# A transformer block with windowed attention: all query blocks through transposed scores, and both feed-forward biases as row products

## The chip, the cores and the metric

The kernel runs on one core of a Trainium2 chip. A core has four compute engines with a queue each: TensorE (PE in the profile; its weight loads are listed apart, as PEld), VectorE (DVE), ScalarE (ACT) and GpSimd (POOL). SyncE (SP) computes nothing here and issues almost all DMAs, in order. The metric is the device time of one execution in microseconds, the median over repeated runs.

## The reference

The input x is 4 sequences of 2048 tokens with 256 channels. What is computed, cut to what matters:

```python
def attn(h):                      # 16 heads of 16 channels, window of 64 keys, causal
    q, k, v = proj(h, Wq), proj(h, Wk), proj(h, Wv)
    bias = where((j <= i) & (j > i - 64), 0, -inf)
    a = softmax(q @ k.T * 0.25 + bias)
    return (a @ v) @ Wo.T

def ffn(h):                       # 1024 hidden units, weights quantized to -1, 0, 1
    return relu(h @ quantize(W1).T + b1) @ quantize(W2).T + b2

x = x + attn(layernorm(x))
x = x + ffn(layernorm(x))
```

Everything is in 32-bit floats. The kernel gets that accuracy from half-precision matmuls by splitting each operand into a high part and a low part (the value minus its high part).

## The kernel before

The 8192 tokens are worked in 32 chunks of 256 (C). A chunk has four query blocks (NB) of 64 tokens, numbered 0 to 3; with the window of 64, a block sees the keys of its own block and of the one before. Heads go in eight pairs (NP).

For each chunk:

- **load** and **norm_in** bring in a chunk (xt), normalize it (layernorm) and transpose its parts by a DMA transpose (xT).
- **project** makes q, k and v. The parts of q and k go to DRAM (qd, kd), and **stack** reads them back into qst and kst so that the rows of one pair of heads lie together for a matmul. The query stack keeps the four blocks interleaved: its columns are in the order (query, block). Three pairs of stacks stand in rotation (NQ), and a pair is loaded again once the chunk three before has signalled "used".
- **scores** computes a block's scores with queries on the rows (sp), eight matmuls of 128 columns. The two key blocks are laid into one half: slot t holds the key of the earlier block where that is still in the window, and otherwise the newer one (copy_predicated, L698). This is the ring order.

From here the blocks take one of two ways. RINGS (L39) says that blocks 0 and 2 of each chunk take the ring path and 1 and 3 the plain one.

- **Ring path, ring_weights (L747 to L793).** VectorE takes the row maxima (L753). The exponentials are made either by one subtraction on VectorE (L764) and one activation (L766), or by eight activations with a bias of their own (L761). ScalarE casts the high part (rh, L771), VectorE or GpSimd subtracts for the low part. VectorE multiplies both parts with two masks that put each slot back to the earlier or the newer key block (pm, L777), and SyncE issues a DMA transpose (pt, L787) that gives the weights with keys on the rows. The stack's use is signalled once for a block, early, behind the scores.
- **Plain path, maxima (L711) and weights (L795).** The row maxima of the chunk's plain blocks are gathered, scaled (mh), transposed on TensorE (L729), copied by ScalarE (mst, L733, one small copy for each block), written to DRAM (md) by a DMA that ScalarE issues and read back by one that GpSimd issues into row 96 of the query stack (L738). Then the scores are computed once more, transposed, with keys on the rows: for a group of four pairs a mask product of 512 columns (L803) and four products of 128 columns whose moving operand is the interleaved query stack (L806). The row maximum is subtracted by the product itself. ScalarE takes the exponential and the high part; the low part is made by GpSimd (L816, L819, L821) or by VectorE out of PSUM (L825, L827, L829). There are two groups to a block, and each signals the stack's use.

**values** (L834) multiplies the weights of a block, from ph and pl or from pt, with v in 24 small products. **wo_out** divides, transposes by DMA, applies Wo, adds to xt and normalizes again. **ffn1** (L955) computes one 128-wide slice of the hidden layer for two chunks together (26 chunks; the last six go one by one), **ffn2** (L1007) the output of a chunk, 32 products, then the sum with xt and the store.

The biases are handled in ffn1 and wo_out:

- First bias: with "folded" false, ScalarE adds it in the ReLU (r, L999), casts the high part (hh, L1002), and the low part is a subtraction on VectorE or GpSimd (hl, L552). With "folded" true, a product with a row of ones puts it into the sum on TensorE (L973), ScalarE makes the ReLU straight into half precision (L991), and VectorE makes the low part out of PSUM (L993).
- Second bias: GpSimd adds it to xt (L944), or TensorE adds it by a row product (L1023).

What sets the order: each piece of work is a generator that says which engine takes it and for about how long. A planner (class Lanes) runs these at build time; of the pieces that could start first, the one with the lowest number goes on (PRIO). The order of issue on each engine that comes out is fixed in the program. **lanes.pick** takes, of several ways to do something, the one that loads the engines most evenly by the planner's own costs; in the program before it never takes "folded", and never TensorE for the second bias.

PSUM: the score tiles sp have two buffers, and all other products share four banks in rotation (BUFS "bank"). The low parts that two engines can make are all in one helper (low, L552), so the profile shows them under one line and tells them apart by their tiles.

Of the kernel before, what the change touches and what calls it, by code (L numbers as in the profile page):

```python
# [23 lines left out]
W = 64  # L24
# [14 lines left out]
RINGS = ((0, 2),)  # L39
RING0 = ()  # L40
NRING0 = 0
PRIO = {'norm': -1.1, 'proj': 0.4, 'max': 0.2, 'att': 2.9, 'val': -2.2, 'wo': 0.6, 'ffn': 5.5, 'ffn2': 5.6, 'prep': 3.6}
BUFS = {'xt': 9, 'ln': 2, 'xT': 3, 'zT': 2, 'qk': 4, 'vp': 4, 'pp': 4, 'op': 2, 'av': 2, 'o': 1, 'h': 10, 'r': 7, 'rh': 1, 'pm': 2, 'pt': 2, 'bank': 4, 'lin': 6, 'sp': 2, 'tp': 3, 'pv': 4}
# [9 lines left out]
class Lanes:  # L53
    """Order of issue: the tasks are generators that say before each piece of work which engine takes it and for
    about how long; of those that could start first, the one with the lowest number goes on. Tasks also wait
    for each other's signals and for buffers."""
# [36 lines left out]
    def pick(self, options):  # L93
        """Of several ways to do something, the one that loads the engines most evenly."""
        top = max(self.load[e] * WT[e] for e in "PADG")
        cost = [sum(t * math.exp((self.load[e] * WT[e] - top) / TAU) for e, t in o) for o in options]
        return cost.index(min(cost))
# [15 lines left out]
    def chain(self, n):  # L113
        """The engines keep the order of issue."""
# [12 lines left out]
    def tensor(self, start, t):  # L127
        """The tensor engine's time for work of t: its clock is halved after a window with little work."""
# [73 lines left out]
def kernel(ctx: ExitStack, tc: tile.TileContext, x, Wq, Wk, Wv, Wo, W1, b1, W2, b2, out):  # L202
# [26 lines left out]
    rhp = pool("rhp", BUFS["rh"])  # L229
    pmp = pool("pmp", BUFS["pm"])  # L230
    ptp = pool("ptp", BUFS["pt"])
# [23 lines left out]
    # channels in the order (channel of a head, pair, head of a pair), so that a stack's rows lie evenly  # L255
# [12 lines left out]
    psh = const.tile([128, 1], FP, name="psh")  # L268
    # stacks: rows 0-95 three parts of 16 channels for each head of a pair, row 96 the row maximum against
    # a constant; the query stack is block diagonal in the heads  # L270
# [3 lines left out]
    b1s = const.tile([128, NF], FP, name="b1s")  # L274
    # biases as rows for the tensor engine: row 0 high part, row 32 low part
    b1r = const.tile([33, FF], HP, name="b1r")
    b2r = const.tile([33, D], HP, name="b2r")
    b2b = const.tile([128, D], FP, name="b2b")
# [6 lines left out]
    sel = const.tile([128, 2, W], HP, name="sel")  # L285
# [4 lines left out]
    xts, xTs, vs, ps_, hs, wts, added = {}, {}, {}, {}, {}, {}, {}  # L290

    # ---- weights and constants

    def constants():
        yield "G", 0.4
        make_identity(nc, ident)
        yield "D", 0.6
        nc.vector.memset(mhalf, -0.5)
        nc.vector.memset(zb, 0.0)
        nc.vector.memset(zh, 0.0)  # L300
        nc.vector.memset(ones, 1.0)
        nc.vector.memset(onesh, 1.0)
        nc.vector.memset(psh, PSHIFT)
        signal("const")
        yield "D", 0.3
        nc.vector.tensor_copy(identh, ident)
        nc.vector.tensor_copy(identb, ident)
        signal("ident")

    def masks():  # L310
        yield wait("ident")
        yield "G", 0.8
        # 1 where slot t still holds the key of the block before (t > q); rows are (head of a pair, query)
        for h in range(2):
            r = slice(h * 64, h * 64 + 64)
            nc.gpsimd.affine_select(sel[r, 0], onesh[r], [[1, W]], ALU.is_gt, 0.0, base=0, channel_multiplier=-1)
        # masks of the transposed scores: rows are keys (64 old, 64 new), columns (pair h q)
# [4 lines left out]
        nc.vector.tensor_scalar(sel[:, 1], sel[:, 0], -1.0, 1.0, ALU.mult, ALU.add)  # L322
        nc.vector.tensor_copy(tri, sel[:, 0])
# [82 lines left out]
    def biases():  # L406
        yield "S", (0.48, 0.45)
        nc.sync.dma_start(out=b1s, in_=b1.rearrange("(c p) -> p c", p=128))
        yield "S", (0.48, 0.36)
        nc.sync.dma_start(out=b2b, in_=b2.partition_broadcast(128))  # L410
# [22 lines left out]
    def weight_f(nm):  # L433
        # the pieces stand in buffers that the chunks need later
# [38 lines left out]
        for i in range(4):  # L473
            # piece i: 2 row blocks x 2 column blocks of 128
# [20 lines left out]
    # ---- the chunks  # L495
# [11 lines left out]
    def layernorm(src):  # L507
        """Gives ht [128, part, half of the channels, NT, 128], parts of the normalized rows of src [128, NT, D]."""
# [34 lines left out]
    def low(args, td, tg):  # L543
        """The low part, on the less loaded of two engines."""
# [22 lines left out]
    def project(c, nm):  # L567
# [60 lines left out]
        if nm == "q":  # L628
            # columns in the order (query, block), as the stack has them
# [8 lines left out]
        # q: high, low, high; k: high, high, low  # L638
# [12 lines left out]
    def stack(c):  # L651
# [26 lines left out]
        for b in range(NB):  # L678
            if b in rings(c):
                start("att", c, ring_weights(c, b), 2 * b)  # L680
            else:
                start("max", c, maxima(c, b), 2 * b)
            start("val", c, values(c, b), b)

    def scores(c, b):
        """Scores of block b: the last half has for each slot the key that the query sees."""
# [14 lines left out]
    def rings(c):  # L701
        return RING0 if c < NRING0 else RINGS[c % len(RINGS)]

    def plains(c):
        return [b for b in range(NB) if b not in rings(c)]

    def used(c):
        if tally(("used", c), len(rings(c)) + 2 * len(plains(c))):
            signal("used", c)

    def maxima(c, b):  # L711
        plain = plains(c)
        ring = yield from scores(c, b)
        yield "D", 0.6
        if ("mx", c) not in ps_:
            ps_["mx", c] = small.tile([128, NP, len(plain)], FP, name="mx")
        mx = ps_["mx", c]
        nc.vector.tensor_reduce(mx[:, :, plain.index(b)], ring, AX.X, ALU.max)  # L718
        put("sp")
        if not tally(("max", c), len(plain)):  # L720
            return
        yield "D", 0.09
        mh = small.tile([128, NP, len(plain)], HP, name="mh")
        nc.vector.tensor_scalar(mh, mx, -1.0 / (SW * SW), PSHIFT * 4.0, ALU.mult, ALU.add)
        yield get("lin")
        yield "P", 0.06 * len(plain)
        mp = lin.tile([NP, len(plain), 128], HP, name="bank")
        for k in range(len(plain)):
            nc.tensor.transpose(mp[:, k, :], mh[:, :, k], identh)  # L729
        yield "A", 0.16 * len(plain)  # L730
        ms = mst[c % NQ]
        for k, b in enumerate(plain):
            nc.scalar.copy(ms[:, :, b], mp[:, k, :])  # L733
# [9 lines left out]
        for b in plain:  # L743
            for g in range(2):
                start("att", c, weights(c, b, g), 2 * b + g)

    def ring_weights(c, b):  # L747
        yield get("r")
        ring = yield from scores(c, b)
        used(c)  # L750
        yield "D", 0.6
        mx = small.tile([128, NP], FP, name="rx")
        nc.vector.tensor_reduce(mx, ring, AX.X, ALU.max)  # L753
        onact = lanes.pick([[("D", 0.6), ("A", 0.48)], [("D", 0.07), ("A", 1.6)]])
        e = rp.tile([128, NP, W], FP, name="r")
        if onact:
            yield "D", 0.07
            nc.vector.tensor_scalar(mx, mx, -0.25 / (SW * SW), PSHIFT, ALU.mult, ALU.add)
            yield "A", 1.6
            for i in range(NP):  # L760
                nc.scalar.activation(e[:, i], ring[:, i], AF.Exp, scale=0.25 / (SW * SW), bias=mx[:, i:i + 1])  # L761
        else:
            yield "D", 0.6
            nc.vector.tensor_tensor(ring, ring, mx.unsqueeze(2).to_broadcast([128, NP, W]), ALU.subtract)  # L764
            yield "A", 0.48
            nc.scalar.activation(e, ring, AF.Exp, scale=0.25 / (SW * SW), bias=psh)  # L766
        put("sp")
        yield get("rh")
        yield "A", 0.52
        rh = rhp.tile([128, 2, NP, W], HP, name="rh")  # L770
        nc.scalar.copy(rh[:, 0], e)  # L771
        yield from low([(rh[:, 1], e, rh[:, 0])], 0.6, 1.11)
        put("r")
        yield get("pm")
        yield "D", 1.14
        pm = pmp.tile([128, 2 * NP, 2, W], HP, name="pm")
        nc.vector.tensor_tensor(  # L777
            pm,
            rh.rearrange("p i a t -> p (i a) t").unsqueeze(2).to_broadcast([128, 2 * NP, 2, W]),
            sel.unsqueeze(1).to_broadcast([128, 2 * NP, 2, W]),  # L780
            ALU.mult,
        )
        put("rh")
        yield get("pt")
        yield "S", (1.4, 1.79)
        pt = ptp.tile([128, 2, NP, 128], HP, name="pt")
        nc.sync.dma_start_transpose(  # L787
            out=pt.rearrange("p i a n -> p (i a) n"), in_=pm.rearrange("p k s t -> p (k s t)")
        )
        put("pm")  # L790
        for g in range(2):
            ps_[c, b, g] = (pt[:, 0, g * 4:g * 4 + 4], pt[:, 1, g * 4:g * 4 + 4])
            signal("p", c, b, g)  # L793
# [40 lines left out]
    def values(c, b):  # L834
# [15 lines left out]
        for g in range(2):  # L850
# [6 lines left out]
            if b not in rings(c):  # L857
                put("pp")
        if b in rings(c):
            put("pt")  # L860
# [31 lines left out]
    def wo_out(c):  # L892
        xt = xts[c]
        # parts of the heads' outputs: rows (head of a pair, query), columns (pair, channel), then transposed
# [41 lines left out]
        added[c] = lanes.pick([[("P", 0.22)], [("G", 1.11)]])  # L936
# [4 lines left out]
        if added[c]:  # L941
            yield wait("biases")
            yield "G", 1.11
            nc.gpsimd.tensor_tensor(xt, xt, b2b.unsqueeze(1).to_broadcast([128, NT, D]), ALU.add)  # L944
        signal("b2", c)

    # chunks that go through the feed-forward layers together
# [130 lines left out]
```

## Time and profile before

| | |
|---|---|
| runs shown | 872.15, 868.52, 870.98 us; median 870.98 |
| profiled execution, span from first to last instruction | 874.9 us |
| mean granted TensorE clock | 0.910 |
| instructions | 21,141 |
| DMA | 143.78 MB in 375,146 packets, 244,257 of them under 512 B |
| queue q1 (SyncE's DMAs) | 83.0% of 16 engines' span |

The costliest rows of each engine in the page's groups (busy time | mean of one) are these:

| engine | row | count | busy us | mean ns |
|---|---|---|---|---|
| VectorE | pm, L777, ring path | 64 | 98.7 | 1541 |
| VectorE | copy_predicated, L698 | 124 | 84.8 | 691 |
| ScalarE | ReLU with bias, L999 | 152 | 92.6 | 630 |
| ScalarE | cast of hh, L1002 | 152 | 81.7 | 566 |
| GpSimd | low part of hl, L552 | 102 | 111.3 | 1104 |
| GpSimd | low part of pl, L821, plain path | 86 | 109.7 | 1283 |
| TensorE | first feed-forward layer, L977 | 608 | 136.1 | 370 |
| TensorE | transposed scores, L806, plain path | 512 | 80.4 | 292 |
| TensorE | mask product, L803, plain path | 128 | 52.8 | 412 |

How to read it: busy time is the union of an engine's instructions. For TensorE the mean of one matmul runs from its start to its modelled end, and the next one starts before that end, so the count times the mean is more than the busy time. A shape such as 128x512 is partitions by elements. In lines of the profile "A <- B" means that A waited for B, or that tile A is written from tile B. In the 40 slices a digit is the busy share in tenths. The profiled execution's span is 3.9 us longer than the median of the runs.

### The profile page before, as it was taken

Reading aid. Unit: us, or ns where it says so; the run is one execution under the profiler, and the core shown is the slowest. Engines: PE = TensorE matmul, PEld = TensorE weight load, DVE = VectorE, ACT = ScalarE, POOL = GpSimd, SP = SyncE. Lnnn points to the kernel's source line nnn. Section 1 sums busy time; section 2 is a strip of 40 time slices with the busy share of each in tenths; the row PEclk is TensorE's granted clock in tenths of the full one; section 3 lists DMA queues with packets and bytes.
Section 4 is the critical chain, followed back from the end, with each engine's and each line's share of the span. In section 5 each row is a group of like instructions: output and inputs, shape, how many; then the busy total and the mean of one; then the engine's idle time right before and its main releaser. Section 6 shows DMA issues by size and latency. Waiting matters only on the chain.

```text
span 874.9 us, 21141 instructions
## 1 busy us (share of the span) xinstructions
PE 711.3 (81%) x8020; PEld 554.0 (63%) x8020; DVE 700.1 (80%) x1262; ACT 589.7 (67%) x1243; POOL 590.3 (67%) x667
## 2 busy tenths in 40 slices
PE   3668787887988798887988888878788979898887
PEld 2457665655757585765856666666665748577765
DVE  6799886488787998789889598787887868787764
ACT  5366888566576858667676567767568577577665
POOL 4436778867667687787768567569757767767652
PEclk9787989898989998998998899899989989989999
DMA  9997999696887998797995969869879998959631
GB/s 212 221 212 160 178 210 178 127 165 128 187 135 170 186 191 182 144 212 132 211 186 106 189 143 192 153 143 190 174 147 190 184 177 159 207 106 156 129 55 49
DMA packets 375146, 143.78 MB, mean 164 GB/s; under 512 B 244257, under 2 KB 372930, under 8 KB 375044
## 3 DMA queue, kind: packets, MB, share of 16 engines
q1 hardware_dynamic: 373508, 141.90, 83.0%
q8 instruction: 63, 1.03, 0.5%
q0 software_dynamic: 1024, 0.26, 0.2%
q10 hardware_dynamic: 512, 0.26, 0.1%
q14 instruction: 39, 0.32, 0.1%
HBM read 40.02 MB, written 33.82 MB: 84 GB/s over the span
## 4 chain that ended last, share of the span: by engine, by line
DVE 31%; PE 21%; DMA 18%; ACT 9%; POOL 8%; issue 8%; SPq 4%; POOLq 0%; ACTq 0%; DVEq 0%
DMA pt<-pm 6%; DVE r L536 5%; DMA xt<-in_dram 4%; DVE pm L777 4%; PE bank L590 4%; PE bank L977 3%; DVE sp L698 3%; DVE st L515 3%; PE sp L693 2%; PE bank L806 2%; DVE hl L636 2%; DMA kst<-kd 2%; PE bank L916 2%; DVE mx L718 2%; POOL o L882 2%
## 5 line engine op out<-in xcount | busy, mean ns | idle before, releaser
L977 PE MATMUL bank<-zT,wq 128*128 128x512 f16 (+1 forms) x608 | 136.1, 370 | 9.6 <-DMA zT<-ht 5.1
L552 POOL TENSOR_TENSOR hl<-r,hh 128x512 f16<-128x512 f32 (+1 forms) x102 | 111.3, 1104 | 33.7 <-ACT hh L1002 27.1
L882 POOL TENSOR_TENSOR o<-av,rec 64x256 f32<-64x256 f32 x128 | 94.2, 737 | 55.7 <-DVE rec L870 48.9
L1025 PE MATMUL bank<-wq,hh 128*128 128x256 f16 x512 | 120.6, 281 | 4.8 <-DVE pl L829 3.4
L1026 PE MATMUL bank<-wq,hl 128*128 128x256 f16 x512 | 120.1, 280 | 0.2 <-POOL hl L552 0.2
L821 POOL TENSOR_TENSOR pl<-r,ph 128x512 f16<-128x512 f32 x86 | 109.7, 1283 | 11.3 <-ACT ph L819 9.9
L698 DVE COPY_PREDICATED sp<-tri,sp 128x512 f32<-128x512 uint8 x124 | 84.8, 691 | 38.2 <-PE sp L693 37.5
L999 ACT ACTIVATE r<-bank,b1s 128x512 f32<-128x512 f32 (+1 forms) x152 | 92.6, 630 | 24.7 <-PE bank L977 21.9
L693 PE MATMUL sp<-kst,qst 96*128 96x128 f16 x1024 | 84.2, 233 | 28.3 <-DMA kst<-kd 22.4
L777 DVE TENSOR_TENSOR pm<-rh,sel 128x2048 f16<-128x2048 f16 x64 | 98.7, 1541 | 9.7 <-POOL rh L552 9.6
L977 PEld LDWEIGHTS <-wq 128*128 128x128 f16 x608 | 59.6, 102 | 59.1 <-issue 20.6
L520 POOL TENSOR_TENSOR rs<-rs,mhalf 128x2 f32<-128x2 f32 x64 | 49.0, 766 | 70.9 <-DVE rs L518 48.4
L693 PEld LDWEIGHTS <-qst 96*128 96x128 f16 x1024 | 74.0, 118 | 34.8 <-issue 25.7
L538 ACT CAST ht<-r 128x512 f16<-128x512 f32 x64 | 40.5, 632 | 75.3 <-DVE r L536 72.4
L552 POOL TENSOR_TENSOR ht<-r,ht 128x512 f16<-128x512 f32 x50 | 62.8, 1255 | 40.0 <-ACT ht L538 32.3
L1002 ACT CAST hh<-r 128x512 f16<-128x512 f32 (+1 forms) x152 | 81.7, 566 | 0.6
L806 PE MATMUL bank<-qst,kst 97*128 97x128 f16 x512 | 80.4, 292 | 0.0
L634 ACT CAST hl<-bank 128x512 f16<-128x512 f32 x64 | 60.5, 961 | 29.0 <-PE bank L590 15.0
L806 PEld LDWEIGHTS <-kst 97*128 97x128 f16 x512 | 56.1, 111 | 37.8 <-issue 22.6
L864 ACT COPY av<-bank 128x272 f32<-128x272 f32 x128 | 50.4, 398 | 43.5 <-PE bank L856 39.5
L636 DVE TENSOR_TENSOR hl<-bank,hl 128x512 f16<-128x512 f32 x64 | 62.2, 997 | 16.9 <-ACT hl L634 15.8
L552 POOL TENSOR_TENSOR rh<-r,rh 128x512 f16<-128x512 f32 x52 | 60.2, 1157 | 21.6 <-ACT rh L771 21.0
(140 smaller groups left out, 2217.0 us busy)
## 6 DMA issues: line engine op xcount, KB each, us to landing
kst<-kd SPq DMA_DIRECT2D x56, 240.0 KB
qst<-qd SPq DMA_DIRECT2D x64, 192.0 KB
xt<-in_dram SPq DMA_DIRECT2D x36, 256.0 KB
qd<-hl SPq DMA_DIRECT2D x32, 256.0 KB
kd<-hl SPq DMA_DIRECT2D x32, 256.0 KB
out_dram<-xt SPq DMA_DIRECT2D x32, 256.0 KB
ve<-vo SPq DMA_DIRECT2D x32, 136.0 KB
qd<-hl SPq DMA_DIRECT2D x32, 128.0 KB
```

The costliest lines, as they stand in the source:

```text
L552: eng.tensor_tensor(o, a, b, ALU.subtract)
L693: nc.tensor.matmul(sp[:, p, :], qs[0:96, p, :, :, b], ks[0:96, p, b * W:b * W + 128], start=True, stop=True)
L698: nc.vector.copy_predicated(sp[:, :, W:128], tri.unsqueeze(1).to_broadcast([128, NP, W]), old)
L777: nc.vector.tensor_tensor(pm, rh.rearrange("p i a t -> p (i a) t").unsqueeze(2).to_broadcast([128, 2 * NP, 2, W]), sel.unsqueeze(1).to_bro ...
L806: nc.tensor.matmul(tp[:, i], ks[0:97, p, b * W:b * W + 128], qs[0:97, p, :, :, b], start=False, stop=i == 3)
L821: nc.gpsimd.tensor_tensor(plf, pf, phf, ALU.subtract)
L882: nc.gpsimd.tensor_tensor(o[r, b0:b0 + 2].rearrange("p b a r -> p (b a) r"), av[r, :, :, h * HD:(h + 1) * HD].rearrange("p b a r -> p (b a ...
L977: nc.tensor.matmul(ps, wq1[:, d, fs], zT[:, i, d, 0:len(grp)], start=n == 0 and not folded, stop=n == 3)
L999: nc.scalar.activation(r[:, 0:n1], ps, AF.Relu, bias=b1s[:, f:f + 1])
L1002: nc.scalar.copy(hh[:, 0:n1], r[:, 0:n1])
L1025: nc.tensor.matmul(ps[:, t, :], hh[:, ts], wq2[:, f, :], start=f == 0 and bool(added[c]), stop=False)
L1026: nc.tensor.matmul(ps[:, t, :], hl[:, ts], wq2[:, f, :], start=False, stop=f == NF - 1)
```

## The change

The ring path is taken out, with its pools and its constants; maxima, weights and values serve all four blocks of a chunk. The maxima of the four blocks are scaled together, transposed in four products and copied in one instruction. "used" counts eight groups of a chunk. The two ways to add the first bias become one, the row product on TensorE; the second bias is always a row product. The loads of the biases in the other forms go. BUFS "pp", the buffers of ph and pl, goes from 4 to 8. Some costs that the planner is told change (0.6 to 0.68 for VectorE, 0.48 to 0.6 for ScalarE in the functions touched).

```diff
-RINGS = ((0, 2),)
-BUFS = {... 'pp': 4, ... 'r': 7, 'rh': 1, 'pm': 2, 'pt': 2, 'bank': 4, ...}
+BUFS = {... 'pp': 8, ... 'r': 7, 'bank': 4, ...}
...
 def stack(c):
         for b in range(NB):
-            if b in rings(c):
-                start("att", c, ring_weights(c, b), 2 * b)
-            else:
-                start("max", c, maxima(c, b), 2 * b)
+            start("max", c, maxima(c, b), 2 * b)
             start("val", c, values(c, b), b)
...
     def used(c):
-        if tally(("used", c), len(rings(c)) + 2 * len(plains(c))):
+        if tally(("used", c), 2 * NB):
             signal("used", c)
...
 def maxima(c, b):
-        mh = small.tile([128, NP, len(plain)], HP, name="mh")
+        mh = small.tile([128, NB, NP], HP, name="mh")
         nc.vector.tensor_scalar(mh, mx, -1.0 / (SW * SW), PSHIFT * 4.0, ALU.mult, ALU.add)
-        for k in range(len(plain)):
-            nc.tensor.transpose(mp[:, k, :], mh[:, :, k], identh)
+        for b in range(NB):
+            nc.tensor.transpose(mp[:, b, :], mh[:, b], identh)
-        for k, b in enumerate(plain):
-            nc.scalar.copy(ms[:, :, b], mp[:, k, :])
+        nc.scalar.copy(ms.rearrange("p q b -> p b q"), mp)
-        for b in plain:
+        for b in range(NB):
             for g in range(2):
                 start("att", c, weights(c, b, g), 2 * b + g)
-    def ring_weights(c, b):
...
 def wo_out(c):
-        added[c] = lanes.pick([[("P", 0.22)], [("G", 1.11)]])
-        if added[c]:
-            nc.gpsimd.tensor_tensor(xt, xt, b2b..., ALU.add)
...
 def ffn1(grp, f):
-        folded = lanes.pick([[("A", 1.1 * k), ("G", 1.11 * k)], [("A", 0.48 * k), ("D", 0.6 * k), ("P", 0.22 * k)]])
-        if folded:
-            nc.tensor.matmul(ps, b1r[:, fs], oner[:, 0:n1], start=True, stop=False)
+        nc.tensor.matmul(ps, b1r[:, fs], oner[:, 0:n1], start=True, stop=False)
-        if folded:
-            ...
-        else:
-            r = rp.tile([128, 2 * C], FP, name="r")
-            nc.scalar.activation(r[:, 0:n1], ps, AF.Relu, bias=b1s[:, f:f + 1])
-            put("lin")
-            nc.scalar.copy(hh[:, 0:n1], r[:, 0:n1])
-            yield from low([(hl[:, 0:n1], r[:, 0:n1], hh[:, 0:n1])], 0.6 * k, 1.11 * k)
+        nc.scalar.activation(hh[:, 0:n1], ps, AF.Relu)
+        nc.vector.scalar_tensor_tensor(hl[:, 0:n1], ps, 0.0, hh[:, 0:n1], ALU.max, ALU.subtract)
+        put("lin")
...
 def ffn2(grp):
-            yield wait("b2", c)
+            yield wait("biases")
-                    if f == 0 and not added[c]:
+                    if f == 0:
                         nc.tensor.matmul(ps[:, t, :], oner[:, 0:128], b2r, start=True, stop=False)
```

## Prediction

> **What bounds the kernel now.** I read the page first: the busy shares, then the 40 slices.
>
> ```profile
> PE 711.3 (81%) x8020; PEld 554.0 (63%) x8020; DVE 700.1 (80%) x1262; ACT 589.7 (67%) x1243; POOL 590.3 (67%) x667
> ...
> PE   3668787887988798887988888878788979898887
> ...
> DVE  6799886488787998789889598787887868787764
> ...
> PEclk9787989898989998998998899899989989989999
> DMA  9997999696887998797995969869879998959631
> ```
>
> No engine is full. TensorE, VectorE and the DMA engines all stand near 80%, with full slices in different places, and the granted clock keeps dipping. So several resources take turns. The chain that ended last says the same:
>
> ```profile
> DVE 31%; PE 21%; DMA 18%; ACT 9%; POOL 8%; issue 8%; SPq 4%; POOLq 0%; ACTq 0%; DVEq 0%
> DMA pt<-pm 6%; DVE r L536 5%; DMA xt<-in_dram 4%; DVE pm L777 4%; PE bank L590 4%; PE bank L977 3%; DVE sp L698 3%; DVE st L515 3%; PE sp L693 2%; PE bank L806 2%; DVE hl L636 2%; DMA kst<-kd 2%; PE bank L916 2%; DVE mx L718 2%; POOL o L882 2%
> ```
>
> TensorE holds only 21% of it. The ring path's own mask product (pm, L777) and transpose (pt) hold 10%. Next, what TensorE waits for (the view of waits: us in total, times, the longest), and what the transposes cost on SyncE's queue (the view of line 787):
>
> ```profile
> PEld L854 <- DMA pt<-pm: 33.9, 22, 3.5
> ...
> PE sp L693 <- DMA kst<-kd: 22.4, 8, 6.3
> ```
> ```profile
> L787 SPq DMA_TRANSPOSE pt<-pm x64: 1566/2918/5030, 61.0 to 826.1; - x64
> ```
>
> The largest wait of TensorE is for the very transposes that go, and each of the 64 holds the one in-order SyncE queue for a median 2.9 us.
>
> **What TensorE's work really takes.** 81% overstates it, since consecutive matmuls overlap. From the timeline of TensorE (start, duration):
>
> ```profile
> 402.37 1.89 PE L977 MATMUL bank<-zT,wq 128*128 128x512 f16 x8
> 404.10 0.38 PE L803 MATMUL bank<-mask,identb 128*128 128x512 bf16 x1
> 404.31 0.63 PE L806 MATMUL bank<-qst,kst 97*128 97x128 f16 x4
> 404.76 0.40 PE L803 MATMUL bank<-mask,identb 128*128 128x512 bf16 x1
> 405.00 0.62 PE L806 MATMUL bank<-qst,kst 97*128 97x128 f16 x4
> ```
>
> Start to start: eight 512-column products take 1.73 us, 0.216 each. A mask product with four transposed scores takes 0.66 us, so each score costs (0.66 - 0.216)/4 = 0.111. In the same stretch twelve 256-column products run from 405.44 to 406.77, 0.110 each; a block's 24 value products from 401.77 to 402.37, 0.60; eight ring-ordered scores 0.45. Times the counts: projections and output 128 groups of twelve, 169; first feed-forward 416 x 0.216 + 192 x 0.110 = 111; second 1024 x 0.110 = 113; transposed scores 128 x 0.66 = 84; values 128 x 0.60 = 77; scores 128 x 0.45 = 58; maxima and preparation 8. That is **620 us** at full clock, 71% of the span of 874.9.
>
> **The change, part by part.** Counts are from the two instruction lists, durations from the groups by form.
>
> *TensorE, added.* The two ring blocks of each of 32 chunks now need two transposed groups each: 128 x 0.66 = 84. Bias rows of the first layer: 104 of 512 columns and 48 of 256, 104 x 0.216 + 48 x 0.110 = 28. Bias of the second: 64 x 0.110 = 7. Transposed maxima: 64 more at 0.057, 4. Values stay 24 products per block, with ph/pl in place of pt. Sum **+123**, so 743 us.
>
> Two rules of the Trainium skill bear on this. "Trainium Kernel Development and Optimization" (Performance Expectations) says that matmul busy time is a bad measure, because matmuls are pipelined. Busy time would give L806 +80.4, L803 +52.8, biases about 49, maxima 9: +191, and 902 us of TensorE alone, slower beyond doubt. Starts give +123, and I take starts. "TensorE: Matmul & The Clock Gate" (Back-to-back issue gap) puts a stream of weight loads and 128-column matmuls at about 81 ns each, 56 without the loads. The 512 added scores would be 41 or 29 us; the row's 0.111 makes 57. Other pairs here (L693) do run at 0.056, so something of the transposed form, whose moving operand steps over four blocks, is slower; I keep the row. By the rule the sum would be +95 to +107.
>
> *VectorE.* Out: the mask products pm 64 x 1.541 = 98.7; subtractions of the maximum 47 x 0.695 = 32.3, or scaled maxima 17 x 0.503 = 8.5; low parts of the hidden layer from SBUF 20.7 + 15.2; ring low parts 12.1; low parts of ht and op that the planner gives to GpSimd, 8 x 0.835 + 7 x 0.847 = 12.6. In: low parts of the hidden layer from PSUM, 104 at the 0.68 of L1031 and 48 at about 0.45 (unseen form: between half of 0.68 and the whole; nearer the SBUF form's 0.596 against 0.909), 92; pl 21 x 0.679 = 14; normalization +3. Sum **-91**: 609 us.
>
> *ScalarE.* Out: ring exponentials 32.5 + 29.3, casts L771 40.8, L999 92.6, L1002 81.7, small copies 23.0, normalization 3.6. In: 107 exponential and cast pairs for GpSimd's route (51.4 + 53.2)/86 = 1.216 each, 130; 21 in place at 1.16, 24; ReLU straight to half precision 104 x 0.60 + 48 x 0.46 = 84; one maxima copy in place of two, 32 x 0.6 (unseen: between L733's 0.487 and 0.63 of a 512-element cast; I take the latter's side, equal free size) 19. Sum **-46**.
>
> *GpSimd.* Out 111.3 (hl), 60.2 (rh), 42.9 (second bias); in pl 107 x 1.283 = 137, ht and op 19. Sum **-58**.
>
> *SyncE and DMA.* Out: 64 transposes at 2.918 = 187 us of queue time, with their waits for pm. Each moves 16 blocks of 128x128 halves, 131,072 packets of 256 B in all; at a mean of 25 ns per such packet in the trace's records over 16 engines, 208 of about 726 us of DMA time. The DMA share falls from 83% to about 59%. Two one-off bias loads go too.
>
> *Added waits.* First, the ring blocks now need the maxima's round trip through DRAM (qst<-md lands after a median 3.7 us); three stacks stand in rotation and blocks of neighbouring chunks fill in, so nothing, at worst 32 x 1 us. The values behind it queue on TensorE, in order. Second, a stack is released only after eight groups, where two of its six signals came early: nothing to 10 us, I take 0; next late would be kst loads (22.4 now). Third, **PSUM banks**: four rotate. A transposed group holds one for a mean 4.0 us from its first matmul to its release in the trace, and 128 are added, 513 us; the folded ReLU holds its bank also through VectorE, about 1.2 us more (0.68 plus hand-over and queue) x 152 = 180. Present holds sum to 2175 us, 62% of four banks; they become some 2870, 82% of the same span. Bounds: -10 us (faster VectorE releases sooner) to +80; the waits of TensorE on bank releasers are now about 30 us, and I take +25.
>
> **The sum.** Of today's 874.9 us TensorE needs 620, loses some 50 to halved clock (0.910 mean granted; all work slowed in proportion would be 61) and idles about 205. Some 45 of the idle are at the ends, before the weights are ready and behind the last outputs; those stay. The pt wait of 34 goes. The other 126 are waits for other engines and loads; TensorE, now late, finds more of its inputs ready: between a quarter and all remain; I take 60%, 76. Clock loss shrinks with the idle, to 20-50; I take 30. Together 743 + 30 + 45 + 76 + 25 = 919 if banks add to the rest; but a bank wait and a late input often coincide, and I take the 25 as inside the 76: **894** of span. The median of the three runs stands 4 us under the profiled span (870.98 against 874.9), so **890 us**, own range 876 to 925.
>
> **Rivals.**
> *TensorE was never the bound, and is simply filled: faster.* For it: the chain has DVE 31%, DMA 18% and TensorE 21%; VectorE, GpSimd, SyncE and DMA all lose work, and the first slices (DMA 9997) sit at the transfers' limit. Against: TensorE ends with 85% of the present span at full clock. Price: 743 + 15 clock + 45 ends + 42 waits = 845 span, 841 us. It decides once clock loss and idle together fall under 132 us (874.9 - 743).
> *Banks decide: much slower.* With four banks 82% claimed and rotated in order, one bank held by a projection (6.7 us from first product to release) stops the next four users. Then 20 of idle are recovered at most and the bank waits come on top: 743 + 45 + 45 + 66 + 60 = 959, so 955 us.
> *No visible change:* idle shrinks by just the added 123. A measurement of this kernel tells about 0.5% from nothing, 866.6 to 875.3.
>
> **How the numbers follow.** The likeliest, a TensorE-bound kernel still starved in places: 0.40. Faster: 0.32. Banks: 0.19. No change: 0.09. Slower is 0.40 + 0.19 = 0.59. Low end 838 (below it a fifth of the faster case), high end 950 (above it rather over half of the banks' case): together under 2 in 10.
>
> **What would show it.** TensorE at 88% or more of its slices and holding over half of the chain; the clock at 0.93 or above; VectorE near 609, ScalarE 544, GpSimd 532 busy; DMA share near 59%; no wait for kst longer than now; more TensorE waits on the releasers of banks. I am wrong if TensorE's chain share stays small, if the transposed scores do not keep 0.111, or if most of the 126 us of waits vanish.

## The result, and the profile after

The changed kernel takes 905.07 us (median of four runs, 897.57 to 909.49) against 870.01 before: **slower, by a ratio of 1.035 (95% interval 1.0304 to 1.0395)**. The quotient of the two medians is 1.040; the ratios here and below come from a separate comparison of the runs and can differ from it by some tenths of a per cent. The forecast was 890 with a range of 838 to 950, and slower at 0.59. The profiled execution is the slowest of the four, with a span of 907.8 us.

The page of the changed kernel, busy shares and slices of the same rows as before:

```profile
PE 834.4 (92%) x8930; PEld 621.2 (68%) x8940; DVE 603.2 (66%) x1231; ACT 583.7 (64%) x1062; POOL 483.6 (53%) x603
...
PE   3669989989989999999999999999999899999997
...
DVE  7877578386763868758675758658585576746553
...
PEclk9779987989979999999999999999999999999999
DMA  9984882573834737374755737584675467361221
```

Now one engine is nearly full. TensorE's row is at eight or nine from the fourth slice to the one before the last, its clock at nine from the 13th slice on (mean 0.964, before 0.910), and every other engine has lost work, ScalarE only 6 us of it. The chain that ended last, by engine and by line:

```profile
PE 60%; DMA 10%; DVE 10%; ACT 7%; issue 5%; SPq 4%; POOL 3%; POOLq 0%; ACTq 0%; DVEq 0%
PE bank L732 10%; PE bank L892 10%; PE bank L929 5%; DMA kst<-kd 5%; PE bank L575 5%; PE sp L675 5%; PE bank L930 5%; PE bank L729 5%; PE bank L888 3%; PE bank L839 3%; PE bank L567 2%; PE bank L782 2%; PE bank L780 2%; PE bank L781 2%; ACT hl L619 2%
```

TensorE had 21% of it before and has 60% now. L732 are the transposed scores, L892 the first feed-forward layer, L888 the new bias rows. Two waits of the kernel before (who waited for what, us in total, times, longest), and those of the changed kernel:

```profile
ACT r L999 <- PE bank L977: 21.9, 18, 5.1
...
PEld L977 <- issue: 20.6, 58, 2.2
```

```profile
ACT hh L905 <- PE bank L892: 95.0, 119, 5.0
...
PEld L892 <- issue: 35.7, 119, 1.0
PEld L888 <- issue: 35.1, 107, 0.8
...
PE sp L675 <- DMA kst<-kd: 10.7, 10, 4.2
```

ScalarE's wait for the first layer's products has grown from 21.9 to 95.0 us, and TensorE's wait for kst has halved. Of the two "issue" lines the one of L888 is new, and that of L892 had 20.6 us before (as L977): on both sides of a bias row the weight load sits with nothing to wait for that the profile shows. The timeline of TensorE shows what that is (start, duration):

```profile
512.31 1.04 PE L892 MATMUL bank<-zT,wq 128*128 128x512 f16 x4
513.28 0.39 PE L888 MATMUL bank<-oner,b1r 33*128 33x512 f16 x1
513.60 1.04 PE L892 MATMUL bank<-zT,wq 128*128 128x512 f16 x4
514.57 0.39 PE L888 MATMUL bank<-oner,b1r 33*128 33x512 f16 x1
```

The four products before the bias row take 0.97 us where 4 x 0.216 is 0.86, and the bias row holds its successor for 0.32 instead of 0.22. A bias product of 33 rows costs 0.10 us on each side beyond its columns. The prediction's sum has none of this.

**An account of TensorE** makes the kernels comparable. Each interval between the starts of two matmuls is held against the pace of its form (0.216, 0.110, 0.112, 0.056, 0.025). The surplus is put down to half clock where the trace has a granted clock of 0.5 in place of 1.0, to the bias rows where it stands beside one and is near 0.1 us, and to waiting otherwise.

| us | work | half clock | bias-row stall | waiting | median time |
|---|---|---|---|---|---|
| before | 619 | 56 | 0 | 189 | 870.01 |
| after | 740 | 21 | 40 | 93 | 905.07 |

The first four columns are of the profiled execution. They leave out 11 us of its span before and 14 after, of which 9 lie ahead of the first matmul and behind the start of the last. So 121 us of work and 40 of stall came in, and 96 of waiting and 35 of half clock were filled up.

### The profile page after: what moved, and what is told of

The parts are those of the page before. It is cut to its first block, busy times and chain, and to the rows that moved or that the text cites. A ratio compares the mean times of both kernels' runs of the same rounds, so it can differ in the third digit from the quotient of the medians.

```text
span 907.8 us, 22598 instructions
## 1 busy us (share of the span) xinstructions
PE 834.4 (92%) x8930; PEld 621.2 (68%) x8940; DVE 603.2 (66%) x1231; ACT 583.7 (64%) x1062; POOL 483.6 (53%) x603
## 3 DMA queue, kind: packets, MB, share of 16 engines
q1 hardware_dynamic: 239204, 108.20, 57.1%
## 4 chain that ended last, share of the span: by engine, by line
PE 60%; DMA 10%; DVE 10%; ACT 7%; issue 5%; SPq 4%; POOL 3%; POOLq 0%; ACTq 0%; DVEq 0%
PE bank L732 10%; PE bank L892 10%; PE bank L929 5%; DMA kst<-kd 5%; PE bank L575 5%; PE sp L675 5%; PE bank L930 5%; PE bank L729 5%; PE bank L888 3%; PE bank L839 3%; PE bank L567 2%; PE bank L782 2%; PE bank L780 2%; PE bank L781 2%; ACT hl L619 2%
## 5 line engine op out<-in xcount | busy, mean ns | idle before, releaser
L747 POOL TENSOR_TENSOR pl<-r,ph 128x512 f16<-128x512 f32 x193 | 220.8, 1158 | 94.7 <-ACT ph L745 78.3
L732 PE MATMUL bank<-qst,kst 97*128 97x128 f16 x1024 | 160.2, 291 | 1.8 <-DMA qst<-md 1.2
L892 PE MATMUL bank<-zT,wq 128*128 128x512 f16 (+1 forms) x608 | 142.1, 357 | 0.9 <-DMA zT<-ht 0.9
L905 ACT ACTIVATE hh<-bank 128x512 f16<-128x512 f32 (+1 forms) x152 | 80.1, 530 | 97.4 <-PE bank L892 95.0
L742 ACT ACTIVATE r<-bank 128x512 f32<-128x512 f32 x193 | 113.9, 601 | 43.8 <-PE bank L732 37.3
L732 PEld LDWEIGHTS <-kst 97*128 97x128 f16 x1024 | 111.8, 110 | 44.1 <-issue 12.7
L745 ACT CAST ph<-r 128x512 f16<-128x512 f32 x193 | 113.5, 624 | 0.4
L907 DVE SCALAR_TENSOR_TENSOR hl<-bank,hh 128x512 f16<-128x512 f32 (+1 forms) x152 | 89.1, 599 | 33.6 <-ACT hh L905 32.8
L729 PE MATMUL bank<-mask,identb 128*128 128x512 bf16 x246 | 97.4, 396 | 6.0 <-ACT av L787 3.0
L675 PE MATMUL sp<-kst,qst 96*128 96x128 f16 x1024 | 76.5, 227 | 19.0 <-DMA kst<-kd 10.7
L892 PEld LDWEIGHTS <-wq 128*128 128x128 f16 x608 | 47.8, 99 | 65.5 <-issue 35.7
L781 PEld LDWEIGHTS <-ph 128*128 128x128 f16 x1024 | 81.1, 97 | 7.6 <-issue 5.5
L780 PEld LDWEIGHTS <-ph 128*128 128x128 f16 x1024 | 83.4, 97 | 1.9
L693 DVE TENSOR_REDUCE mx<-sp 128x8 f32<-128x512 f32 x128 | 83.4, 679 | 0.1
```

Source lines behind the costliest of these rows:

```text
L675: nc.tensor.matmul(sp[:, p, :], qs[0:96, p, :, :, b], ks[0:96, p, b * W:b * W + 128], start=True, stop=True)
L729: nc.tensor.matmul(tpf, identb, msk.rearrange("p a q -> p (a q)"), start=True, stop=False)
L732: nc.tensor.matmul(tp[:, i], ks[0:97, p, b * W:b * W + 128], qs[0:97, p, :, :, b], start=False, stop=i == 3)
L742: nc.scalar.activation(pf, tpf, AF.Exp, scale=0.25 / (SW * SW))
L745: nc.scalar.copy(phf, pf)
L747: nc.gpsimd.tensor_tensor(plf, pf, phf, ALU.subtract)
```

## The experiments

Three theories stood against each other. **A:** TensorE's own work and stalls set the time. **B:** the four PSUM banks, held longer, are what it waits for. **C:** the maxima's round trip through DRAM and the later release of a stack hold things up. Each run is compared with the kernel before on the same chip, whose medians were 871.41, 871.90 and 872.24 us in the three groups of runs.

### The bias rows, and the parts of the change alone

e1_full_rows is the changed kernel with

```diff
-    b1r = const.tile([33, FF], HP, name="b1r")
-    b2r = const.tile([33, D], HP, name="b2r")
-    oner = const.tile([33, 2 * C], HP, name="oner")
+    b1r = const.tile([128, FF], HP, name="b1r")
+    b2r = const.tile([128, D], HP, name="b2r")
+    oner = const.tile([128, 2 * C], HP, name="oner")
```

> The changed kernel, its two bias products given all 128 rows (the added rows are zeros in the bias and change no sum). Theory A, TensorE's own work sets the time: in the changed kernel's trace a bias product of 33 rows starts about 0.10 us later than its neighbours' pace allows, and the product behind it waits 0.10 us more (0.319 from start to start in place of 0.216), 216 x 0.2 = 43 us in all. With full rows this goes: TensorE keeps the 0.216 and 0.110 pace, and the time falls by 30 to 43 us, to 862 to 875. Theory B, the four PSUM banks are what it waits for: TensorE goes faster but stops for banks, 895 to 905. Theory C, the maxima's round trip through DRAM and the later release of the stacks: unchanged, 900 to 908.

Measured: **880.61 us**, ratio 1.0116 (1.0048 to 1.0184). Its timeline:

```profile
502.05 0.38 PE L888 MATMUL bank<-oner,b1r 128*128 128x512 f16 x1
502.26 1.02 PE L892 MATMUL bank<-zT,wq 128*128 128x512 f16 x4
503.13 0.38 PE L888 MATMUL bank<-oner,b1r 128*128 128x512 f16 x1
503.34 1.03 PE L892 MATMUL bank<-zT,wq 128*128 128x512 f16 x4
```

From bias row to bias row it is 1.08 us, where the changed kernel has 1.29. The stall is gone, and 24.5 of its 40 us come back as time; half clock falls to 13, and waiting rises from 93 to 105. That is somewhat less than theory A's 30 to 43: part of the stall had covered other waits.

e2_paths_only is the kernel before with `RINGS = ((),)` and eight buffers pp; both biases stay where they were.

> The kernel before with every block on the transposed path and nothing else (eight buffers pp as in the change); the biases stay with ScalarE and GpSimd. TensorE has 620 + 84 + 4 = 708 us of work by starts, where the changed kernel has 743 and 43 of stalls at the bias rows. Theory A: 845 to 870, the whole loss or more comes from the bias rows. Theory B: 128 more holds of a bank of 4 us each are all still there, three quarters of what was added: 885 to 900. Theory C: the round trip and the late release are all there: 900 to 908.

Measured: **920.22 us**, ratio 1.0539 (1.0453 to 1.0625), slower than the whole change and above what any of the three theories allowed. Theory A fails here: TensorE has 708 us of work and no bias rows, where the changed kernel has 740 and 40 of stall, and it waits 163 us against 93. More than its own work is at play.

e3_bias_only is the kernel before, ring path and all, with

```diff
-        folded = lanes.pick([[("A", 1.1 * k), ("G", 1.11 * k)], ...])
+        folded = True
...
-        added[c] = lanes.pick([[("P", 0.22)], [("G", 1.11)]])
+        added[c] = 0
```

> The kernel before with its ring path, and with both biases always as row products. TensorE 620 + 35 + 43 for the rows = 698 us. Theory A: more work on an engine that is not alone the bound, while VectorE, the SyncE queue and the DMAs stay as full as before: 875 to 895. Theory B: 152 bank holds longer by 1.2 us, a quarter of what was added: 878 to 885. Theory C: 866 to 874, as before.

Measured: **866.70 us**, ratio 0.9945 (0.9922 to 0.9968): no loss, and by the interval a gain of about half a per cent. Theories A and B expected a loss here and miss; no change is what C expected. TensorE got 35 us of work and 40 of stall and lost nothing by it: its waiting fell from 189 to 129 and its half clock from 56 to 29. In exchange VectorE went from 700 to 658 us busy and GpSimd from 590 to 529.

The loss seems to be the path's and not the biases'. But neither run changes its half alone. There are two routes for the low part of the attention weights, by GpSimd and by VectorE, and the planner chose anew: of the 128 transposed groups of the kernel before it sends 42 by VectorE, of those of e3_bias_only none, and of the 256 of e2_paths_only 204. By the runs that follow a group on VectorE's route costs 0.2 to 0.3 us, so that some 10 us of what the bias rows seem to bring may come from the route; a run with the biases alone and the routes held was not made. And the path alone loses more than both together; the next runs ask why.

### Which engine makes the low part

In e2_paths_only the planner sends the low part of the weights to VectorE in 204 of 256 groups, since GpSimd has the hidden layer's low parts; in the changed kernel it is 63. On VectorE's route a group keeps its bank through two passes of ScalarE and one of VectorE, on GpSimd's only through the first pass. e6_short_holds is e2_paths_only with

```diff
-        if lanes.pick([[("D", 0.6), ("A", 0.96)], [("G", 1.11), ("A", 1.0)]]):
+        if True:
...
-            yield from low([(hl[:, 0:n1], r[:, 0:n1], hh[:, 0:n1])], 0.6 * k, 1.11 * k)
+            yield "D", 0.6 * k
+            nc.vector.tensor_tensor(hl[:, 0:n1], r[:, 0:n1], hh[:, 0:n1], ALU.subtract)
```

> The kernel with only the paths changed (920.2 us), the low part of the attention weights always made by GpSimd from SBUF, so that a transposed group gives its bank back after one activation, and the low part of the hidden layer always by VectorE. There 204 of the 256 groups were on VectorE's route and held their bank for a mean 4.2 us. Theory B, bank holds are what that kernel waits for: the hold falls to about 2.4 us and the time to 880 to 895. Rival, ScalarE with 645 us of work in a fixed order is: the route changes nothing for ScalarE, 912 to 925. By theory A, with the same TensorE work: 912 to 925.

Measured: **873.76 us**, ratio 1.0018 (0.9991 to 1.0046). The 46 us are gone, with the same work on TensorE, and the time lies below even theory B's 880 to 895. ScalarE is no rival: it is busy 645 us in both. TensorE's waiting fell from 163 to 126. The same pair of extremes on the changed kernel with full rows, with `if True:` in e11_all_gpsimd and `if False:` in e12_all_vector in place of the same choice:

> The changed kernel with full bias rows (880.6 us), the low parts of all 256 transposed groups made by GpSimd (193 of them now), which gives a bank back after one activation. If the holds of the banks still matter there: 865 to 876, with less idle on TensorE. If the 63 on VectorE's route do no harm: 878 to 890.

> The same with the low parts of all 256 groups made by VectorE out of PSUM, a bank held through two passes of ScalarE and one of VectorE. ScalarE and TensorE have the same work, GpSimd 223 us less, VectorE some 130 us more. If the time follows the hold of the banks (with only the paths changed, 204 groups on this route cost 46 us against none): 915 to 935, the hold near 4.2 us. If not: 878 to 890, as no engine is full at that: VectorE would have about 730 of 880 us.

Measured: **872.66 us** (ratio 1.0002, 0.9979 to 1.0026) and **947.76 us** (1.0845, 1.0782 to 1.0908). The busy shares of e12_all_vector:

```profile
PE 822.4 (87%) x8916; PEld 646.8 (68%) x8940; DVE 653.2 (69%) x1362; ACT 625.6 (66%) x1168; POOL 276.7 (29%) x419
```

No engine is full, and yet it is the slowest kernel of the study. Side by side, with the time from a group's first transposed score to the release of its bank, taken from the records:

| | groups on VectorE's route | mean hold, us | TensorE waiting | half clock | time |
|---|---|---|---|---|---|
| e11_all_gpsimd | 0 of 256 | 1.49 | 101 | 14 | 872.66 |
| e1_full_rows | 63 | 2.14 | 105 | 13 | 880.61 |
| e12_all_vector | 256 | 4.02 | 155 | 40 | 947.76 |
| e6_short_holds | 0 | 2.15 | 126 | 28 | 873.76 |
| e2_paths_only | 204 | 3.94 | 163 | 38 | 920.22 |

The time follows the route in both families, and the hold of the bank goes with it. Theory B's range was met in e11_all_gpsimd; in e6_short_holds and e12_all_vector the effect was larger than its range. What TensorE waits for agrees in part. Three of its waits in e12_all_vector:

```profile
PE bank L780 <- DVE pl L755: 8.1, 17, 1.3
PE bank L729 <- ACT av L787: 7.8, 13, 1.0
...
PE bank L729 <- DVE pl L755: 5.5, 13, 0.8
```

L729 is the mask product and L780 a value product, and neither reads pl or av: by the profile's releasers they wait for a bank. All such waits of over 0.15 us together are 28 us in e11_all_gpsimd and 58 in e12_all_vector, 34 in e6_short_holds and 57 in e2_paths_only. That is rather over half of the 54 and 37 us by which TensorE's waiting differs. The route also moves work between engines and lets the planner write another order, and in e6_short_holds it moves the hidden layer's low parts as well. That it is the bank alone, and not VectorE's turn in the chain, is not shown.

### The round trip and the stacks

e8_nq4 is e1_full_rows with `NQ = 4` (and seven buffers pp in place of eight).

> The changed kernel with full bias rows (880.6 us), four stacks in rotation in place of three (and seven buffers pp in place of eight, for space). Theory C, the later release of a stack holds up the loads of the next one: the waits of the scores for kst (14 us) go, and the time falls by 10 us or more, under 871. Theories A and B: within 876 to 885.

Measured: **881.75 us**, ratio 1.009 (1.0067 to 1.0113), the same as with three stacks. The waits for kst, which were to go, rose from 14.2 to 22.1 us. So a fourth stack brings nothing, and theory C falls in that part. The round trip itself was not tried alone, but in the changed kernel TensorE waits only 1.2 us for what comes back from it:

```profile
PE bank L732 <- DMA qst<-md: 1.2, 1, 1.2
```

GpSimd, which issues the read, waits 38.9 us for md, where it waited 28.3 before.

### Why a transposed score takes 0.112 us

e4_k128 is the changed kernel with

```diff
-            nc.tensor.matmul(tp[:, i], ks[0:97, ...], qs[0:97, p, :, :, b], ...)
+            nc.tensor.matmul(tp[:, i], ks[0:128, ...], qs[0:128, p, :, :, b], ...)
```

and the added rows set to zero once at the start.

> The changed kernel, its transposed scores taken over 128 rows of the stacks, the rows 97 to 127 set to zero once. If the 97 rows make a transposed score take 0.111 us from start to start where the ring-ordered ones of 96 rows take 0.056, it falls to 0.056, TensorE loses 1024 x 0.055 = 56 us of work and by theory A the time falls to 850 to 865. If it is the step of four elements in the moving operand, the pace stays 0.11 and the time stays at 900 to 908. Theories B and C: 900 to 908 either way.

Measured: **913.71 us**, ratio 1.0497 (1.0433 to 1.0561), and a score still takes 0.116 us at the median. The row count is not it. That the time lies above the 900 to 908 that were expected is not explained; the planner's order is another one here too, with 70 groups on VectorE's route in place of 63.

e7_block_major is e1_full_rows with the stack's columns in the order (pair, block, head, query), so that the moving operand is contiguous.

```diff
-    qst = [const.tile([128, NP, 2, W, 4], HP, name=f"qst{i}") for i in range(NQ)]
+    qst = [const.tile([128, NP, 4, 2, W], HP, name=f"qst{i}") for i in range(NQ)]
...
-    ... qs[0:97, p, :, :, b] ...
+    ... qs[0:97, p, b] ...
```

> The changed kernel with full bias rows (880.6 us), the query stack laid out with a block's 128 columns together in place of interleaved with step four; the projection writes q in natural order, the stack's loads come in runs of 128 B in place of 512 B. If the step in the moving operand makes a transposed score take 0.112 us from start to start, it falls to 0.056 and TensorE loses 57 us: theory A 835 to 855. If the step isn't it, the pace stays at 0.11 and the time near 880; theories B and C 875 to 885 either way. The loads of q cost four times the packets: if the DMAs are then in the way, waits for kst and qst grow and the gain is smaller.

Measured: **884.40 us**, ratio 1.0123 (1.0094 to 1.0152): no gain, although the cause was right. The timeline of e1_full_rows, with 0.67 us from one mask product to the next, and then that of this run:

```profile
506.07 0.38 PE L729 MATMUL bank<-mask,identb 128*128 128x512 bf16 x1
506.29 0.62 PE L732 MATMUL bank<-qst,kst 97*128 97x128 f16 x4
506.74 0.40 PE L729 MATMUL bank<-mask,identb 128*128 128x512 bf16 x1
```
```profile
516.91 0.38 PE L727 MATMUL bank<-mask,identb 128*128 128x512 bf16 x1
517.13 0.39 PE L730 MATMUL bank<-qst,kst 97*128 97x128 f16 x4
517.35 0.38 PE L727 MATMUL bank<-mask,identb 128*128 128x512 bf16 x1
```

A group takes 0.44 us, 0.055 for a score. TensorE lost 56 us of work (740 to 684), but waits 150 us where it waited 105, and another 21 went to half clock. TensorE's waits name the new limit, e1_full_rows first:

```profile
PE sp L675 <- DMA kst<-kd: 14.2, 10, 3.7
```
```profile
PE sp L673 <- DMA kst<-kd: 51.0, 27, 4.0
```

The stack's loads now come in 128 B runs, and q1's share of the DMA engines, 59.1% in e1_full_rows, is 66.8% here.

e9_step_two and e10_ring_step_two go half way: blocks interleaved in twos, runs of 256 B.

```diff
+    qst = [const.tile([128, NP, 2, 2, W, 2], HP, name=f"qst{i}") for i in range(NQ)]
...
+    ... qs[0:97, p, b // 2, :, :, b % 2] ...
```

> The changed kernel with full bias rows (880.6 us), blocks of the query stack interleaved in twos, so that the moving operand of a transposed score steps over two elements in place of four, and the stack's loads come in runs of 256 B in place of 512 B (128 B with the blocks apart, where 57 us less on TensorE ended as 37 us more of waiting for kst and 884.4 us). If TensorE and the loads share the bound, as that run suggests, and the pace at step two is 0.056 us: kst waits of 14 to 30 us and 850 to 872. If the pace stays at 0.11: 878 to 890.

Measured: **858.41 us**, ratio 0.9846 (0.9794 to 0.9898), faster than the kernel before by 1.5%, in the range where TensorE and the loads share the bound. At a step of two a score takes 0.057 us, so the whole gain of pace is there, and 22 of its 56 us reach the time; waiting for kst, 37.6 us where 14 to 30 were expected, stands between and leads the chain's lines:

```profile
PE 38%; DMA 19%; DVE 17%; ACT 7%; SPq 6%; issue 6%; POOL 5%; POOLq 0%; ACTq 0%; DVEq 0%
DMA kst<-kd 12%; PE bank L892 6%; PE sp L675 4%; PE bank L929 4%; PE bank L930 4%; PE bank L575 4%; DVE sp L680 3%; PE bank L732 3%; DVE mx L693 2%; DMA xt<-in_dram 2%; PE bank L839 2%; POOL pl L747 2%; DVE r L521 2%; PE bank L567 2%; PE bank L729 2%
```

### The best of both

e5_ring_full_rows is e3_bias_only with the full rows of e1_full_rows: ring path for two blocks, both biases on TensorE.

> The kernel before with its ring path and both biases as row products, these now of 128 rows. By starts TensorE has 654 us of work; the run with 33 rows added 40 us of stalls at the bias rows and ended at 866.7. Theory A, TensorE's work and stalls set the time by part: of the 40 us about six tenths come back, as with all blocks transposed (24.5 of 40): 840 to 852. If TensorE isn't the bound with the ring path, as the run with 33 rows suggests (78 us more on TensorE and no loss), the stalls were filled from other waits: 860 to 868.

Measured: **849.22 us**, ratio 0.9727 (0.9696 to 0.9759), the fastest kernel here. The busy shares and the chain:

```profile
PE 718.4 (85%) x8229; PEld 563.8 (66%) x8236; DVE 657.1 (77%) x1260; ACT 564.1 (67%) x1287; POOL 525.9 (62%) x609
```
```profile
PE 33%; DVE 20%; DMA 18%; ACT 11%; POOL 8%; issue 7%; SPq 3%; POOLq 0%; DVEq 0%; ACTq 0%
PE bank L977 7%; DMA pt<-pm 7%; PE bank L590 4%; DMA xt<-in_dram 3%; DMA kst<-kd 3%; PE sp L693 3%; DVE pm L777 3%; PE bank L1025 3%; PE bank L1026 3%; PE bank L806 3%; DVE sp L698 2%; POOL pl L821 2%; ACT r L761 2%; DVE hl L636 2%; PE bank L973 2%
```

Nothing is full, and no engine holds more than a third of the chain. Of the 40 us of stall 17.5 came back, within theory A's range and outside its rival's: the stalls were not all filled from other waits. Against the kernel before this run too has none of its groups on VectorE's route, where that one has 42, so that the 22 us may not all be the bias rows'.

> The kernel before with both biases as full row products (849.2 us), with the same step of two. TensorE loses up to 28 us, but the DMAs here are loaded with the ring path's transposes as well: if the loads are what it waits for, 849 to 865; if TensorE's work is, 835 to 847.

Measured: **852.61 us**, ratio 0.9761 (0.9701 to 0.9821), not to be told from e5_ring_full_rows. Here 28 us less of work on TensorE is worth nothing: q1's share is 89.2%, and 25.8 us of waiting for pt and 23.1 for kst remain.

## Why the prediction was right, and where its sum was off

**The direction and the bound** were right: TensorE takes over (chain 21% to 60%, busy 92%, clock 0.964 with 0.93 or more expected), VectorE and the DMAs are relieved as priced (603 us with 609 expected, DMA share 57.1% with 59%), and the kernel is slower. What makes it slower was not what the sum had kept, as the last paragraph of this part says.

**TensorE's work** was right: 743 us were worked out from starts and 740 are measured; busy time would have had 902. The transposed score kept the row's 0.112, and not the 0.081 or 0.056 that the prediction weighed from the Trainium skill ("TensorE: Matmul & The Clock Gate", Back-to-back issue gap); the ring-ordered scores, each with a weight load of its own, run at 0.056. The reason that was guessed, the moving operand's step, is confirmed: contiguous or with a step of two, the same product takes 0.055 to 0.057.

**The bias rows are the term that was mis-sized.** They were priced by their columns, 35 us; with the stall of about 0.1 us before and after each of the 216 they take 75. By the run with full rows this put 24.5 us on the time, more than the whole miss of 15 us (905 against 890).

**Waiting and clock** were set too high, which hid most of that: 45 + 76 of waiting against 107 measured (the 93 of the account and the 14 us of span outside it), 30 of half clock against 21. The forecast span was 743 + 30 + 121 = 894; measured are 740 + 40 + 21 + 107 = 908. That the number came so near is in part luck.

**The banks** came out the other way. More waits of TensorE on the releasers of banks were expected, 25 us more. Added up over the waits of more than 0.15 us, they are some 60 us in the kernel before, where the prediction read about 30, and 27 after. A transposed group, counted from its first score, held its bank 3.76 us before and 2.14 after (the prediction's 4.0 counts from the mask product), so 256 groups hold 548 us where 128 held 481, and not 513 more. The folded first layer holds its bank 0.7 us longer (3.03 to 3.75), with 1.2 expected. That holds matter is supported by the runs, but their length depends on the route that the planner picks, and the prediction did not weigh that. It put 63 groups on VectorE's, worth 8 us by the run without any; 204 of them, in the kernel with the paths alone, are worth 46, with the hidden layer's low parts moved as well.

**The added waits** that were priced at nothing: of the later release of the stacks no cost shows (881.75 with four, 880.61 with three), and the wait for kst fell, to 10.7 us, as expected. The round trip was not isolated; TensorE waits 1.2 us for it.

**Rows of other engines.** ScalarE was expected at 544 us and takes 584. The maxima's one copy was priced at 0.6 us and takes 1.29 (L707, 41.3 us in all), which is 22 of the 40. The rest lies in adding up groups that overlap: the busy times of ScalarE's groups, added, fell by 35 us (674 to 639), and the busy time of the engine only by 6. GpSimd came out at 484 us where 532 was expected, since its instructions got faster (below).

Taken together by the runs, 905.07 less 24.5 for the bias rows and 8 for the 63 groups is 872.6, which is the time of e11_all_gpsimd and of the kernel before (that one with 42 groups on VectorE's route). In e11_all_gpsimd TensorE's 121 us of added work are paid for in full by what the change relieves: against the kernel before, waiting is down from 189 us to 101, and half clock from 56 to 14. The work still counts, since 56 us less of it in e9_step_two gave 22 us. The prediction's likeliest case came about, but the loss that was left over came from the stalls at the bias rows and from the route of 63 groups, not from the waits that the sum had kept. That the direction came out so clearly is luck to that extent: without the stalls the loss is 1.2%, and with all groups on GpSimd's route there is none.

## What to carry to other kernels

Price a matmul by the interval between starts of its own form, rows and step of the moving operand included; a product of 33 rows between neighbours of 128 cost more than its columns. When one path is removed from a kernel whose planner balances by engine load, look at which route the remaining work then takes and how long it keeps a PSUM bank: the choice of route moved this kernel by 75 us, and no engine was full in the slower one. And try the halves of a change by themselves: here one half lost 5.4% and the other, mended, gained 2.7%. Hold the planner's other choices while doing so; here they moved along, and blur what each half is worth.

## What the runs showed of the hardware

- A product with 33 rows between products of 128 rows started about 0.10 us late and held its successor 0.10 us more: 0.319 us from start to start for 512 columns and 0.212 for 256, against 0.216 and 0.109 with 128 rows. Products of 96 and 97 rows between those of 128 show nothing of the size.
- A moving operand in half precision with a step of four elements takes 0.098 to 0.116 us for 128 columns, with steps of two and one 0.055 to 0.058. In windows of half clock the stepped one takes the same 0.116, and those with steps of two and one go to 0.107, so at a step of four it is not TensorE's clock that sets the pace. The same step in the stationary operand (the ring-ordered scores) left the pace at 0.056.
- GpSimd's subtraction for pl is slower beside the ring path's mask product on VectorE (pm). In the kernel before it takes a mean 1283 ns: 1627 for the 21 that overlap a mask product in time, 1172 for the other 65. With that product it takes 1281 to 1303 in the runs, without it 1158 to 1168, but 1204 in e6_short_holds, where VectorE makes the hidden layer's low parts from SBUF.
